# A graph layer on one core: loads first in SyncE's queue, norms of two blocks interleaved, early rows kept in later left factors

## The chip, the core and the metric

The kernel runs on one core of a Trainium2 chip. The metric is the device time of one execution in microseconds (us); the median of three runs before the change is 1426.39 us. A profile of one further execution is read beside it.

A core has several engines, each with its own queue of instructions that it works off in order: TensorE (PE; its weight loads are listed as PEld), VectorE (DVE), ScalarE (ACT), GpSimd (POOL) and SyncE (SP), which here only issues DMAs. An instruction that has to wait holds up everything behind it on its engine.

## The reference

```python
# x: (1250, 1024), 20000 edges (src -> dst, type 0..7), D = 1024
h = relu(layernorm(x))                     # per row, no scale or shift
u = h @ root + bias
for r in range(8):
    mask = (edge_type == r)
    sums = segment_sum(h[src] * mask, dst)
    cnt  = segment_sum(mask, dst)
    u = u + (sums / max(cnt, 1)) @ weight[r]
z = concat([u, h]) @ w_gate + b_gate
out = x + tanh(u) * z + h * (1 - z)
```

The data are float32. So 11 matrices of 1024 x 1024 are applied to 1250 rows: eight edge types, root, and the two halves of the gate.

## The kernel before, in words

The 1250 rows are ten blocks of 128 (the last has 98). Blocks i and i + 5 form a pair; NP = 5 pairs. One step multiplies one pair by one matrix, and there are 11 x 5 = 55 steps. A step is written as a two by two scheme with seven half-size products instead of eight, each of them four matrix instructions (two records apiece in the profile). The left operands of the seven products, `A11, A12, A22, S1, S2, S3, S4`, are seven slots of one tile `h_op[i]` for each pair; `transposed` (L171) fills the A slots by transposing h on TensorE into PSUM banks and copying (one half on ScalarE, one on VectorE, L179), and `left` (L183) forms S1 to S4 on VectorE. The right operands are sums of the matrix's four quarters; `make_t1` to `make_t4` (L157 to L169) form them on VectorE. `product` (L192) runs the seven products and their evacuations: with banks b and c, the first goes into b, and b is copied out by ScalarE (L210); the second goes into c (L213); the third is ADDED to what lies in b and copied out (L216); the fourth is added to c (L219 on VectorE); the fifth to b (L223, L224); the sixth has bank a (L228); the seventh is added to b (L231). After each product a function `between` may put other work into the queues; that is one turn of the generators below.

The engines' queues other than GpSimd's are in the order in which the Python program issues the instructions; the buffer pools add waits where a buffer is taken again.

The start: x is loaded by SyncE (`load_x`, L359) into three rotating buffers `xt`; `normed` (L366) takes the statistics of a block on VectorE (L370, L372), a square root on ScalarE (L374), the scale on VectorE (L376, L378) and a ReLU on ScalarE (L380), and stores h (L381); `with_h` (L383) adds h to x and stores the sum (L386), which frees the x buffer. h of pairs 0 to 3 is held in `lend`, two slots of the last pair's left factor, free until that pair is transposed. Pair 0 is done before the first step; the generator `norms` (L684) does pairs 1 to 4 during the first steps, 15 turns in all. Beside it the generator `columns` (L421) loads the edges, fills a table in memory and computes an integer key for every edge. After both, `slots` (L500) ranks the edges in 40 groups of up to 512 (two turns each; L534 and L585 on TensorE, L613 scatters to the table from GpSimd), and `order` (L630) sorts the nodes by their number of edges: L643 broadcasts 30 x 128 values, L667 compares them, and `rows_and_weights` (L331) writes the node order (L334), reads it back (L343) and gathers each node's slots (L298). From step 20 on, `edges` (L773) gathers result rows by GpSimd (L753) and adds them on VectorE (L761) between the products of later steps. Results of a step are stored by SyncE (L274) from four rotating buffers.

Of the kernel before, what the change touches and what calls it, by code (L numbers as in the profile page):

```python
# [19 lines left out]
def tile_rgcn_highway(  # L20
# [331 lines left out]
    with ExitStack() as early:  # L352
# [6 lines left out]
        def load_x(i, part):  # L359
            d = i + part * NP  # L360
            n = nrows(d)
            t = xpool.tile([P, D], F32, name="xt")
            nc.sync.dma_start(t[:n], x[d * P:d * P + n, :])
            return t

        def normed(xt, ht, d):  # L366
            n = nrows(d)
            st = xpool.tile([P, 2, 6], F32, name="st")
            for j in range(2):
                nc.vector.bn_stats(st[:n, j, :], xt[:n, j * Q:(j + 1) * Q])  # L370
            mv = xpool.tile([P, 2], F32, name="mv")
            nc.vector.bn_aggr(mv[:n], st[:n].rearrange("p a b -> p (a b)"))  # L372
            sd = xpool.tile([P, 1], F32, name="sd")
            nc.scalar.activation(sd[:n], mv[:n, 1:2], AF.Sqrt, bias=eps[:n])  # L374
            rs = xpool.tile([P, 1], F32, name="rs")
            nc.vector.reciprocal(rs[:n], sd[:n])  # L376
            less = xpool.tile([P, 1], F32, name="less")
            nc.vector.scalar_tensor_tensor(less[:n], mv[:n, 0:1], -1.0, rs[:n],  # L378
                                           op0=OP.mult, op1=OP.mult)
            nc.scalar.activation(ht[:n], xt[:n], AF.Relu, scale=rs[:n], bias=less[:n])  # L380
            nc.sync.dma_start(h_dram[d * P:d * P + n, :], ht[:n])  # L381

        def with_h(xt, ht, d):  # L383
            n = nrows(d)
            nc.vector.tensor_add(xt[:n], xt[:n], ht[:n])  # L385
            nc.sync.dma_start(xh_dram[d * P:d * P + n, :], xt[:n])  # L386


        lend = [h_op[NP - 1][:, 2 * part:2 * part + 2].rearrange("p a k f -> p (a k f)")
                for part in range(2)]  # L390
        xs = [load_x(0, 0), load_x(0, 1)]
        fac[0].load_first()
        fac[0].load_b22()
        fac[0].load_b21()
        xs.append(load_x(1, 0))
        for part in range(2):
            normed(xs[part], lend[part], part * NP)
        for part in range(2):
            transposed(h_op[0], part, lend[part], nrows(part * NP))
# [4 lines left out]
        left(h_op[0], 3)  # L404
        fac[0].make_t4()
        for part in range(2):
            with_h(xs.pop(0), lend[part], part * NP)
        xs.append(load_x(1, 1))


# [10 lines left out]
        def columns():  # L421
            with tc.tile_pool(name="ix0", bufs=1) as ix0:
                far = ix0.tile([P, G * ND * WIDE // 4], I32, name="far")
                nc.gpsimd.memset(far, FAR)
                for t in table.rearrange("(a p f) o -> a p (f o)", a=4, p=P):
                    nc.sync.dma_start(t, far)

                C2 = NCH - P
                ed, f = {}, {}
                for name, of, pad in (("dst", dst, G * KEYS), ("typ", etype, R), ("src", src, 0)):  # L430
                    t = ix0.tile([P, 2, P], I32, name=f"e_{name}")
                    nc.gpsimd.memset(t[:, 1, :], pad)
                    nc.sync.dma_start(t[:, 0, :], of[:P * P].rearrange("(c p) -> c p", p=P))
                    nc.sync.dma_start(t[:C2 - 1, 1, :],
                                        of[P * P:(NCH - 1) * P].rearrange("(c p) -> c p", p=P))
                    nc.sync.dma_start(t[C2 - 1:C2, 1, :EL], of[None, (NCH - 1) * P:])
                    ed[name] = t
                yield
                for name in ("dst", "typ", "src"):
                    f[name] = ix0.tile([P, 2, P], F32, name=f"f_{name}")  # L440
                    nc.vector.tensor_copy(f[name], ed[name])
                late = ix0.tile([P, 2, P], F32, name="late")
                nc.vector.tensor_single_scalar(late, f["typ"], float(R0[1]), op=OP.is_ge)
                for g in range(2, G):
                    nc.vector.scalar_tensor_tensor(late, f["typ"], float(R0[g]), late,
                                                   op0=OP.is_ge, op1=OP.add)
                key = ix0.tile([P, 2, P], F32, name="key")
                nc.vector.scalar_tensor_tensor(key, late, float(KEYS), f["dst"],
                                               op0=OP.mult, op1=OP.add)
                key_i = ix0.tile([P, 2, P], I32, name="key_i")  # L450
                nc.vector.tensor_copy(key_i, key)
                lo_i = ix0.tile([P, 2, P], I32, name="lo_i")
                nc.vector.tensor_single_scalar(lo_i, key_i, P - 1, op=OP.bitwise_and)
                for to, of in ((keys_dram, key_i), (los_dram, lo_i)):
                    nc.sync.dma_start(to[:P * P].rearrange("(c p) -> c p", p=P), of[:, 0, :])
                    nc.sync.dma_start(to[P * P:].rearrange("(c p) -> c p", p=P), of[:C2, 1, :])
                yield

                blk_i = ix0.tile([P, 2, P], I32, name="blk_i")
                nc.vector.tensor_single_scalar(blk_i, ed["dst"], 7, op=OP.arith_shift_right)  # L460
                blk = ix0.tile([P, 2, P], F32, name="blk")
                nc.vector.tensor_copy(blk, blk_i)
                row = ix0.tile([P, 2, P], F32, name="row")
                nc.vector.scalar_tensor_tensor(row, f["typ"], float(N), f["src"],
                                               op0=OP.mult, op1=OP.add)
                for g in range(1, G):
                    less = late
                    nc.vector.tensor_scalar(less, f["typ"], float(R0[g]),
                                            float((R0[g - 1] - R0[g]) * N),
                                            op0=OP.is_ge, op1=OP.mult)  # L470
                    nc.vector.tensor_add(row, row, less)
                tb = ix0.tile([P, 2, P], F32, name="tb")
                nc.vector.scalar_tensor_tensor(tb, f["typ"], float(ND), blk,
                                               op0=OP.mult, op1=OP.add)
                yield
                yield

                for of, to in ((key, key_col), (row, row_col), (tb, tb_col)):
                    p = bank()
                    nc.tensor.transpose(p[:, :P], of[:, 0, :], ident)  # L480
                    nc.tensor.transpose(p[:, P:P + C2], of[:C2, 1, :], ident[:C2, :C2])
                    nc.vector.tensor_copy(to, p[:, :NCH])
                yield
                kcol_i = ix0.tile([P, NCH], I32, name="kcol_i")
                nc.vector.tensor_copy(kcol_i, key_col)
                part_i = ix0.tile([P, NCH], I32, name="part_i")
                nc.vector.tensor_single_scalar(part_i, kcol_i, P - 1, op=OP.bitwise_and)
                nc.vector.tensor_single_scalar(less_lo, part_i, -1.0, op=OP.mult)
                nc.vector.tensor_single_scalar(part_i, kcol_i, 7, op=OP.arith_shift_right)
                nc.vector.tensor_copy(hi_col, part_i)  # L490
                nc.vector.tensor_single_scalar(first, key_col, float(WIDE), op=OP.mult)
                nc.gpsimd.iota(io, pattern=[[1, P]], base=0, channel_multiplier=0,
                               allow_small_or_imprecise_dtypes=True)
                nc.gpsimd.iota(pid, pattern=[[0, 1]], base=0, channel_multiplier=1,
                               allow_small_or_imprecise_dtypes=True)
                nc.vector.tensor_scalar(before, io, pid, None, op0=OP.is_lt)
                nc.vector.tensor_single_scalar(less_pid, pid, -1.0, op=OP.mult)
                yield
# [131 lines left out]
        def order():  # L630

            with tc.tile_pool(name="sort", bufs=1) as sp:
# [48 lines left out]
                for _ in range(3):  # L681
                    yield

        def norms():  # L684
            for i in range(1, NP):
                yield
                hs = []
                for part in range(2):
# [9 lines left out]
                if i < NP - 1:  # L698
                    for part, (xt, ht, d) in enumerate(hs):
                        transposed(h_op[i], part, ht, nrows(d))  # L700
# [400 lines left out]
```

## Time and profile before

| what | us |
|---|---|
| median of the runs | 1426.39 (1426.23 to 1426.68) |
| the profiled execution, its own time | 1420.9 |
| its span in the trace | 1419.1 |
| TensorE busy | 1369.2 |
| VectorE busy | 862.2 |
| GpSimd busy | 610.9 |
| ScalarE busy | 338.5 |

The mean granted clock of TensorE was 0.987 of full speed. In the profile a line such as L201 is a line of the kernel; a group's row names the tile written, the tiles read, the shape, the number of instructions and their duration. An arrow `<-` behind an idle time names what ended it. In the rows for stretches of time, the columns are the stretch, the busy time of PE, PEld, DVE, ACT and POOL, the granted clock, the share of the DMA engines that was busy, and GB/s.

### The profile page before, as it was taken

Reading aid. Unit: us, or ns where it says so; the run is one execution under the profiler, and the core shown is the slowest. Engines: PE = TensorE matmul, PEld = TensorE weight load, DVE = VectorE, ACT = ScalarE, POOL = GpSimd, SP = SyncE. Lnnn points to the kernel's source line nnn. Section 1 sums busy time; section 2 is a strip of 40 time slices with the busy share of each in tenths; the row PEclk is TensorE's granted clock in tenths of the full one; section 3 lists DMA queues with packets and bytes.
Section 4 is the critical chain, followed back from the end, with each engine's and each line's share of the span. In section 5 each row is a group of like instructions: output and inputs, shape, how many; then the busy total and the mean of one; then the engine's idle time right before and its main releaser. Section 6 shows DMA issues by size and latency. Waiting matters only on the chain.

```text
span 1419.1 us, 11950 instructions
## 1 busy us (share of the span) xinstructions
PE 1369.2 (96%) x3562; PEld 619.3 (44%) x3562; DVE 862.2 (61%) x1658; ACT 338.5 (24%) x718; POOL 610.9 (43%) x537
## 2 busy tenths in 40 slices
PE   5789999999999999999999999999999999999996
PEld 2344444444444444444444444444444444444442
DVE  5754877797768805077545663745446464567983
ACT  1234565566631111110101111111111111121210
POOL 0000665565561648474534343445425333324531
PEclk9799999999999999999999999999999999999998
DMA  7563765476646146467957655887769644557751
GB/s 253 202 223 96 154 170 128 109 174 161 134 101 195 35 76 150 120 227 272 320 206 242 230 188 186 277 317 254 252 250 321 219 149 169 192 180 270 265 162 56
DMA packets 109863, 272.73 MB, mean 192 GB/s; under 512 B 25890, under 2 KB 27920, under 8 KB 109664
## 3 DMA queue, kind: packets, MB, share of 16 engines
q0 software_dynamic: 48864, 128.60, 27.6%
q1 hardware_dynamic: 39808, 101.38, 23.9%
q10 hardware_dynamic: 21120, 41.95, 9.6%
q8 instruction: 28, 0.46, 0.2%
q14 instruction: 43, 0.35, 0.1%
HBM read 214.20 MB, written 80.65 MB: 208 GB/s over the span
## 4 chain that ended last, share of the span: by engine, by line
PE 80%; issue 6%; DVE 4%; DMA 1%; POOL 1%; ACT 0%; POOLq 0%; DVEq 0%; ACTq 0%
PE ps L201 79%; PE ps_n L534 1%; DVE row L1052 1%; DVE row L1053 0%; DMA got<-h_dram,node 0%; DVE w L990 0%; DVE h_op L990 0%; DMA y<-row 0%; PE ps_q L585 0%; DVE u L954 0%; PE ps L177 0%; POOL out_dram L303 0%; DVE row L228 0%; POOL got L298 0%; DVE u L761 0%
## 5 line engine op out<-in xcount | busy, mean ns | idle before, releaser
L201 PE MATMUL ps<-w,h_op 128*128 128x512 f32 x3080 | 1345.1, 596 | 1.0 <-ACT row L210 1.0
L201 PEld LDWEIGHTS ps<-w,h_op 128*128 128x128 f32 x3080 | 580.7, 191 | 695.7 <-issue 690.8
L753 POOL DMA_INDIRECT got<-y,idx x202 | 249.8, 1237 | 279.6 <-DVE u L761 226.1
L761 DVE SCALAR_TENSOR_TENSOR u<-got,w_of,u 128x1024 f32<-128x1024 f32 (+1 forms) x192 | 245.9, 1282 | 132.5 <-DMA got<-y,idx 130.4
L613 POOL DMA_INDIRECT table<-row_col,at_i x157 | 176.4, 1124 | 160.9 <-DVE at_i L609 68.5
L219 DVE TENSOR_TENSOR row<-row,ps 128x512 f32<-128x512 f32 x55 | 37.7, 686 | 164.7 <-PE ps L201 135.3
L223 ACT COPY part<-ps 128x512 f32<-128x512 f32 x55 | 32.1, 584 | 277.2 <-PE ps L201 269.7
L231 ACT COPY row<-ps 128x512 f32<-128x512 f32 x50 | 29.2, 584 | 259.7 <-PE ps L201 247.1
L224 DVE TENSOR_TENSOR row<-row,part 128x512 f32<-128x512 f32 x55 | 37.9, 689 | 65.5 <-ACT part L223 56.7
L210 ACT COPY row<-ps 128x512 f32<-128x512 f32 x55 | 32.1, 583 | 173.3 <-PE ps L201 155.0
L213 ACT COPY row<-ps 128x512 f32<-128x512 f32 x55 | 32.1, 583 | 137.4 <-PE ps L201 128.7
L216 ACT COPY row<-ps 128x512 f32<-128x512 f32 x55 | 32.1, 583 | 129.6 <-PE ps L201 126.9
L599 DVE SCALAR_TENSOR_TENSOR junk<-k_bc,key_col,before 128x128 f32<-128x128 int32 x157 | 54.9, 349 | 4.2
L334 POOL DMA_INDIRECT node_dram<-ids,pos_i x30 | 36.2, 1206 | 38.8 <-issue 38.2
L157 DVE TENSOR_TENSOR w<-w,w 128x2048 f32<-128x2048 f32 x11 | 25.3, 2298 | 44.7 <-PE ps L201 44.7
L228 DVE TENSOR_TENSOR row<-row,ps 128x512 f32<-128x512 f32 x55 | 37.6, 683 | 24.2 <-PE ps L201 22.5
L516 ACT ACTIVATE is_lo<-io,less_lo 128x128 bf16<-128x128 f32 x157 | 50.1, 391 | 0.8 <-DMA xh_dram<-xt 0.8
L539 DVE TENSOR_TENSOR seen<-seen,ps_n 128x110 f32<-128x110 f32 x157 | 42.1, 268 | 12.8 <-PE ps_n L534 8.1
L667 DVE SCALAR_TENSOR_TENSOR junk<-v_bc,val,one 128x1280 bf16<-128x1280 f32 x30 | 46.5, 1551 | 3.9 <-DMA v_bc<-val_dram 3.1
L303 POOL DMA_INDIRECT u_dram<-u,node x20 | 25.7, 1285 | 51.8 <-DVE u L761 38.3
L181 POOL MEMSET h_op<- 128x120 f32 x4 | 0.8, 200 | 89.0 <-DVE xt L385 88.8
L177 PE MATMUL ps<-ident,h_op 128*128 128x128 f32 x64 | 12.1, 351 | 27.5 <-ACT h_op L380 27.3
(153 smaller groups left out, 752.5 us busy)
## 6 DMA issues: line engine op xcount, KB each, us to landing
y<-row SPq DMA_DIRECT2D x72, 512.0 KB
w<-in_L_gnn_weight_dram ACTq DMA_DIRECT2D x28, 1024.0 KB
k_bc<-keys_dram SPq DMA_DIRECT2D x39, 256.0 KB
l_bc<-los_dram SPq DMA_DIRECT2D x39, 256.0 KB
w<-in_L_gnn_w_gate_dram ACTq DMA_DIRECT2D x8, 1024.0 KB
xt<-in_x_dram SPq DMA_DIRECT2D x9, 512.0 KB
xh_dram<-xt SPq DMA_DIRECT2D x9, 512.0 KB
hr_dram<-row SPq DMA_DIRECT2D x9, 512.0 KB
```

The costliest lines, as they stand in the source:

```text
L201: nc.tensor.matmul(b, aop[:, i, k, :], w.of[i][:, k, :], start=(fresh and k == 0), stop=(k == KQ - 1), skip_group_check=True)
L219: nc.vector.tensor_add(c12, c12, c)
L224: nc.vector.tensor_add(c22, c22, d)
L228: nc.vector.tensor_add(c11, c11, a)
L334: ins = nc.gpsimd.indirect_dma_start(out=node_dram[g][:, :], out_offset=bass.IndirectOffsetOnAxis(ap=pos_i[:, g, d:d + 1], axis=0), in_=id ...
L516: nc.scalar.activation(is_lo[:, i, :], io, AF.Abs, bias=less_lo[:, c0 + i:c0 + i + 1])
L539: nc.vector.tensor_add(seen[j][:, i, :], was, p[:, i, :])
L599: nc.vector.scalar_tensor_tensor(junk, o["k_bc"][:, i, :], key_col[:, c:c + 1], before, op0=OP.is_equal, op1=OP.mult, accum_out=rank[:, c: ...
L613: ins = nc.gpsimd.indirect_dma_start(out=table[:, :], out_offset=bass.IndirectOffsetOnAxis(ap=at_i[:n, i:i + 1], axis=0), in_=row_col[:n, ...
L667: nc.vector.scalar_tensor_tensor(junk, v_bc[:, g, :], val[:, c:c + 1], one.to_broadcast([P, KEYS]), op0=OP.is_gt, op1=OP.mult, accum_out=p ...
L753: nc.gpsimd.indirect_dma_start(out=t[:n], out_offset=None, in_=y[g][:, :], in_offset=bass.IndirectOffsetOnAxis(ap=at[:n, d, k:k + 1], axis=0),
L761: nc.vector.scalar_tensor_tensor(u[:n], t[:n], w, u[:n], op0=OP.mult, op1=OP.add)
```

## The change

SyncE's queue begins with x of pair 0, the first matrix's quarters with x of pair 1 put among them, one block of pair 2, then the edges and the table. The stores of h and of x + h come after them. x of pair 1 goes into `h_op[3]` (slots of pair 3's left factor) instead of the rotating buffers, and h of pair 1 into free slots of `h_op[4]` and `h_op[3]`. The norms of a pair's two blocks interleave (`both`): the second block's first statistics stand between the first block's square root and its scale. Pair 0's ReLU is issued in two halves, and a square root of a constant stands first in ScalarE's queue. The norm of pair 1 is issued before the first step; its transposes come after the first step's fifth product instead of its fourth. `norms` now takes 18 turns, and `columns` lets six turns pass before it begins to compute.

```diff
@@ the norm of a block in parts (stats, spread, scale, relu, store, with_x), and of two blocks @@
+        def both(a, b, parts=1):
+            a.stats(0)
+            a.stats(1)
+            a.spread()
+            b.stats(0)
+            a.scale()
+            a.relu(parts)
+            b.stats(1)
+            b.spread()
+            b.scale()
+            b.relu(parts)
+
+        def factored(i, blocks):
+            for part in range(2):
+                transposed(h_op[i], part, blocks[part].ht, blocks[part].n)
@@ the start @@
-        xs = [load_x(0, 0), load_x(0, 1)]
+        warm = xpool.tile([P, 1], F32, name="warm")
+        nc.scalar.activation(warm, eps, AF.Sqrt)
+        x0 = [load_x(0, part) for part in range(2)]
         fac[0].load_first()
         fac[0].load_b22()
+        x1 = [load_x(1, 0, scratch(NP - 2, 0))]
         fac[0].load_b21()
-        xs.append(load_x(1, 0))
-        for part in range(2):
-            normed(xs[part], lend[part], part * NP)
-        for part in range(2):
-            transposed(h_op[0], part, lend[part], nrows(part * NP))
+        x1.append(load_x(1, 1, scratch(NP - 2, 1)))
+        xs = [load_x(2, 0)]
...
+        b0 = [Normed(part * NP, x0[part], scratch(NP - 1, part)) for part in range(2)]
+        both(*b0, parts=2)
+        factored(0, b0)
         fac[0].make_t1()
         left(h_op[0], 1)
         fac[0].make_t2()
         fac[0].make_t3()
         left(h_op[0], 3)
+        b1 = [Normed(1 + part * NP, x1[part], scratch(NP - 1 - part, 2)) for part in range(2)]
+        both(*b1)
         fac[0].make_t4()
-        for part in range(2):
-            with_h(xs.pop(0), lend[part], part * NP)
-        xs.append(load_x(1, 1))
+        for b in b0 + b1:
+            b.store()
+        for b in b0:
+            b.with_x()
+        xs += [load_x(2, 1), load_x(3, 0)]
@@ columns: the loads of the edges and the table are issued above, before b0 @@
+            for _ in range(6):
+                yield
@@ norms @@
-            for i in range(1, NP):
+            for _ in range(4):
                 yield
...
+            factored(1, b1)
+            left(h_op[1])
+            yield
+            for b in b1:
+                b.with_x()
+            yield
+            for i in range(2, NP):
+                blocks = []
+                if i < NP - 1:
+                    blocks = [Normed(i + part * NP, xs.pop(0), scratch(NP - 1, part))
+                              for part in range(2)]
+                    both(*blocks)
                     yield
+                    for b in blocks:
+                        b.store()
                     yield
+                    factored(i, blocks)
+                    left(h_op[i])
+                    yield
+                    for b in blocks:
+                        b.with_x()
+                    xs.append(load_x(i + 1, 1))
+                    if i + 2 < NP:
+                        xs.append(load_x(i + 2, 0))
+                    yield
...
@@ index @@
-            for _ in zip_longest(columns(), norms()):
+            for _ in zip_longest(norms(), columns()):
                 yield
```

Line numbers in the prediction are those of the kernel before.

## The prediction

> **What bounds the kernel now.** I read the share of each engine first, then TensorE's waits, then windows of 5 us over the start, then the timelines of the places where TensorE stood. Page, parts 1 and 2:
>
> ```profile
> PE 1369.2 (96%) x3562; PEld 619.3 (44%) x3562; DVE 862.2 (61%) x1658; ACT 338.5 (24%) x718; POOL 610.9 (43%) x537
> PEclk9799999999999999999999999999999999999998
> ```
>
> TensorE is busy for 1369.2 of 1419.1 us, so only its 49.9 idle us and its slow clock can be won. By windows of 20 us it idles 9.2, 12.3, 5.4, 0.6, 4.2 and 2.6 us in the first 120 us (34.3), then hardly until the end. Who ends that idle time (TensorE's waits, 0 to 130 us: total, times, longest), and the windows (columns: span, busy of PE, PEld, DVE, ACT, POOL, clock, DMA):
>
> ```profile
> PE ps L177 <- ACT h_op L380: 27.3, 4, 14.8
> PE ps L177 <- ACT xt L380: 6.8, 2, 4.2
> 25.00:30.00 5.00, 2.72 (x7) 0.94 (x5) 2.46 (x3) 0.00 (x0) 0.00 (x0) 1.00 0.53 210
> 30.00:35.00 5.00, 0.00 (x0) 0.00 (x0) 0.00 (x0) 0.00 (x0) 0.00 (x0) 0.68 0.81 220
> 35.00:40.00 5.00, 0.00 (x0) 0.00 (x0) 3.50 (x10) 0.00 (x0) 0.00 (x0) 0.50 0.13 33
> 50.00:55.00 5.00, 5.00 (x13) 2.17 (x11) 2.78 (x6) 0.59 (x1) 0.00 (x0) 0.77 0.98 330
> ```
>
> All of it is transposes (L177) waiting for a normalised block (L380). The clock falls to half about 4.1 us after the last matmul (27.73; 0.68 in 30 to 35 puts the fall at 31.8) and returns 3.2 us after matmuls resume (49.13; 0.77 in 50 to 55 puts it at 52.3). Timelines (start, duration, engine; in brackets idle before):
>
> ```profile
> 5.69 1.28 ACT L374 ACT_TABLE_LOAD   x1 [5.69 <-DVE mv L372]
> 9.09 4.04 PE L177 MATMUL ps<-ident,h_op 128*128 128x128 f32 x16 [9.09 <-ACT h_op L380]
> 12.92 14.81 PE L201 MATMUL ps<-w,h_op 128*128 128x512 f32 x32
> 17.46 0.58 ACT L210 COPY row<-ps 128x512 f32<-128x512 f32 x1 [4.57 <-PE ps L201]
> 42.56 1.97 PE L177 MATMUL ps<-ident,h_op 128*128 128x128 f32 x8 [14.84 <-ACT h_op L380]
> 49.13 5.17 PE L201 MATMUL ps<-w,h_op 128*128 128x512 f32 x8
> 105.45 13.92 PE L201 MATMUL ps<-w,h_op 128*128 128x512 f32 x32
> 119.21 0.36 PE L534 MATMUL ps_n<-is_at,is_lo 128*128 128x110 bf16 x4
> ```
>
> TensorE is out of work at 27.73 and resumes at 42.56. One of the seven products of a step is 8 records, 3.45 us warm, 5.17 us from cold. Each ScalarE copy of a finished product (L210) runs as soon as the product is done. A later place has no margin either, and I weigh it because the change moves the index work:
>
> ```profile
> 458.69 1.55 POOL L334 DMA_INDIRECT node_dram<-ids,pos_i  x1 [29.85 <-issue]
> 594.82 1.02 POOL L753 DMA_INDIRECT got<-y,idx  x1 [0.30 <-issue]
> 598.99 1.28 DVE L761 SCALAR_TENSOR_TENSOR u<-got,w_of,u 128x1024 f32<-128x1024 f32 x1 [31.38 <-DMA got<-y,idx]
> 608.37 0.58 ACT L210 COPY row<-ps 128x512 f32<-128x512 f32 x1 [5.79 <-DMA y<-row]
> 609.01 16.58 PE L201 MATMUL ps<-w,h_op 128*128 128x512 f32 x38 [0.98 <-ACT row L210]
> ```
>
> GpSimd works without a wait on TensorE from 458.69 (first node rows) to 594.82 (fifth gather). VectorE stands in order behind that gather for 31.4 us; the row store behind it is late, so is the copy L210, and TensorE stops for 0.98 us. Margin: none.
>
> **The start.** The same ten x loads, ten h stores, ten x+h stores, nine edge loads and four table stores are issued; SyncE now puts x of block pairs 0 and 1, one block of pair 2, the edges and the table ahead of the stores. ScalarE gets one dummy square root, and two ReLUs become four halves. Bytes up to the last x of pair 1: 6.3 MB; at the 341 GB/s of the first 20 us, landed by about 18.5, before VectorE wants it.
>
> First block pair: the table load leaves the chain (row: 1.28 us, the square root follows at 6.98 at once). ScalarE: Activation LUTs, section What ACT_TABLE_LOAD costs, counts a drain of about 1.38 beside the load, 2.66 together; that would give 1.4 us more. The row decides: 1.28. Statistics of the second block lie beside the first's square root, and halves of ReLU let transposes begin at about 7.4. Last transpose 11.4, against 13.1; first product from 11.2 instead of 12.92 and, with the same ramp, over at 15.8. Second product to 19.25.
>
> Here stands a new wait. On ScalarE, both ReLUs of pair 1 now stand AHEAD of L210, and the third product accumulates into the bank that L210 reads. VectorE: right-factor and left-factor sums 12.1 to 21.2 (2.2 and 0.6 to 0.7 each, as at 13.77 to 22.9 before), statistics and scales of pair 1 to 25.85 (0.64 each, 0.21, 0.16, square root 0.3, with the second one behind the first ReLU of 1.24), so the second ReLU ends at 27.1, L210 at 27.7. Behind the ReLUs in ScalarE's queue stand L210, L213, L216 and matrix 1's first two loads; for L210 the third product waits, for L213 the fourth. Third product: 27.75 instead of 19.25. TensorE idles 8.5 us, goes cold, and the product takes 5.05 instead of 3.45.
>
> From there, chained: fourth 36.25, fifth 39.7 (ReLUs long done), 16 transposes 41.8, sixth 45.3, seventh 48.7. VectorE waits for the fourth product to 36.3, then follows with margin. Step 1: products to 55.65; transposes of pair 2 (its ReLUs end 54.3) to 57.75; third 61.2; six index transposes 1.24; fourth to sixth 72.8; transposes of pair 3 (last x load is issued 2.7 us after the x+h store of pair 2, as at 57.49 and 60.16 before, landing 69.2; second ReLU ends 73.5) to 74.9; seventh 78.35. Step 2: second product 85.25; 0.7 us wait for the ReLU of pair 4, whose target buffer is freed by a store; 87.0; fourth 93.9; transposes 94.65; fifth 98.1. That is where the row of 119.21 stands (19 products done): gain 21.1 us. Check from the other side: idle 25.1 after the first transposes, about 6.2 of slow clock (two sets and one of 8 transposes at 1.97 for 1.04, two products 1.7 over) and 1.7 of start are 33.0; less 8.5, 1.6 and 0.7 are 22.2. I take 21.1.
>
> The price of the moves on other queues: matrix 1's loads on ScalarE are issued near 33 instead of 46 and used a whole matrix later; GpSimd's fill of the short block waits nowhere that matters; stores at SyncE now wait behind loads, and their first reader comes in the gate.
>
> **The index.** Norms take 18 turns instead of 15 before the edge groups begin: the first group (L534) comes after 22 products, not 19; the last after 105, not 102. In TensorE's own time the chain to GpSimd is up to 10.3 us later. Worked on the time of before: last group's product at 433.2 instead of 422.4; VectorE is less behind, its result at 434.6 (before 426.8); last scatter and the wait for it to 440.1 (430.3): 9.8 late. Then the broadcast of 1.92 MB (L643), which landed 7 us after its issue at 433.33 with nothing beside it, is issued at 443.1, at the same time as the two 1 MB weight loads of ScalarE's queue (443.27). The row, alone on the engines, would add nothing. DMA: Bandwidth & Descriptors, section Queues, rings and completion order, says that each engine takes turns between its queues packet by packet, which speaks against the change here: shared equally, 1.9 MB beside 1.9 MB take about twice the 5 us of data, 4.5 more. The row would make the whole cost 9.8 + 1.6 = 11.4, the rule 15.9. No row of before has the two together; I take the middle, 2.2. Ten L667 follow, then the node rows: GpSimd's chain starts 12.0 late and ends 12.0 late. The margin being none, TensorE stops 12.0 us longer, and the clock falls: 1.6 more. Cost 13.6. TensorE doesn't wait between 119 and 608 otherwise, and what comes after is paced by it.
>
> Sum: 21.1 - 13.6 = 7.5 us off. Against the profiled execution, 1420.9 us (span 1419.1) to 1413.4; the runs' median, 1426.39, stands 5.5 above that, so 1418.9; I say 1419.
>
> **Rivals.**
> Cover holds: the index delay doesn't reach TensorE. It would need slack in GpSimd's chain; only its 29.85 us wait before 458.69 is slack, and that is for VectorE's places, which are late themselves. Then only the start counts: 1426.4 - 21.1 = 1405.3. Chance 0.17.
> The ScalarE order doesn't bite: the third product starts at 19.3. Then 10.1 more: 1409; with the first rival 1395. The order of ScalarE's queue speaks against it. 0.05.
> More waits at the start (pair 3's late x, VectorE with hardly any idle time between 12 and 30): 4 to 8 us lost, 1423 to 1427, about no change. 0.11.
> Slower: GpSimd's wait for its node-row scatters. For group 0 it was 3.65 us (473.3 to 478.2), for the others 12.0 and 10.3. Should group 0's become 12.0 at its new place, beside the row stores, with the broadcast shared equally (4.5), the chain is 9.8 + 4.5 + 8.3 = 22.6 us late, plus 1.6: 24.2 against 21.1, 1429.5. It decides from a chain 19.5 us late. 0.07.
>
> **How the numbers follow.** Forecast 0.60: 1419, its own range 1415 to 1423 (broadcast 0 or 4.5, the start 2 either way). The range for 8 in 10 takes in the first rival and the better of the second: 1404 to 1423.5. A measurement can tell 0.2%, 2.85 us, from none: faster below 1423.5, slower above 1429.2. Faster: 0.59 of the forecast, 0.22 of the first two; 0.01 of the forecast and most of the waits are the same; faster 0.81, same 0.11, slower 0.08.
>
> **What would show it.** First transposes near 7.4. In the start ONE TensorE gap of about 8.5 us from 19 to 28, ended by ScalarE's L210, with the clock at 0.5 by its end; no other gap over 1.5 us; first index matmul after 22 products. At GpSimd the fifth gather later relative to TensorE by 12, and a TensorE gap of about 13 us where 0.98 was. Wrong would be: no gap at 19 (the second rival), a gap of about 1 us at the gather (the first), or an end of GpSimd's chain over 19 us late (the last).

## The result, and the profile after

The changed kernel takes 1408.01 us (median of 6 runs, 1403.13 to 1412.53), the kernel before 1426.11 (6 runs, 1423.66 to 1426.68). The ratio is 0.9875 (95% interval 0.9853 to 0.9897): 18.1 us off, where 7.5 were forecast. The profiled run of the changed kernel took 1409.36 us (span 1407.5), that of before 1420.9.

Page of the changed kernel, parts 1 and 2:

```profile
PE 1369.5 (97%) x3562; PEld 617.6 (44%) x3562; DVE 862.2 (61%) x1658; ACT 339.0 (24%) x721; POOL 624.3 (44%) x537
PEclk8999999999999999999999999999999999999998
```

TensorE's busy time is what it was (1369.2); its idle time fell from 49.9 to 38.0 us. Its waits over the whole span (line waited for, total, times, longest):

```profile
PE ps L201 <- ACT row L210: 8.5, 2, 8.2
PE ps L177 <- ACT h_op L400: 7.8, 2, 7.6
PE ps L201 <- DVE row L228: 5.8, 1, 5.8
PE ps L902 <- DVE most L899: 2.1, 1, 2.1
PE ps L177 <- ACT xt L400: 0.8, 1, 0.8
PE ps_q L636 <- ACT to_lo L627: 0.3, 1, 0.3
```

Of 34.1 us of transposes that waited for a norm (L177, first two lines of before), 8.6 are left, and 7.6 of these are the very first block's. In their place stand two waits on products: L210 at the start and L228 at the fifth gather. Timelines of the changed kernel, TensorE and then ScalarE, over the start (start, duration, engine; in brackets idle before):

```profile
7.55 4.01 PE L177 MATMUL ps<-ident,h_op 128*128 128x128 f32 x16 [7.55 <-ACT h_op L400]
11.35 7.81 PE L201 MATMUL ps<-w,h_op 128*128 128x512 f32 x16
27.32 13.56 PE L201 MATMUL ps<-w,h_op 128*128 128x512 f32 x24 [8.16 <-ACT row L210]
40.72 1.91 PE L177 MATMUL ps<-ident,h_op 128*128 128x128 f32 x16
```

```profile
23.71 1.24 ACT L400 ACTIVATE h_op<-h_op,less,rs 128x1024 f32<-128x1024 f32 x1 [0.52 <-DVE less L393]
25.56 1.24 ACT L400 ACTIVATE h_op<-h_op,less,rs 128x1024 f32<-128x1024 f32 x1 [0.42 <-DVE less L393]
26.71 0.56 ACT L210 COPY row<-ps 128x512 f32<-128x512 f32 x1
27.17 0.58 ACT L213 COPY row<-ps 128x512 f32<-128x512 f32 x1
```

The first product was done near 15 (in the first experiment below, where nothing stands ahead of it, its copy runs at 14.99), but L210 stands behind pair 1's two ReLUs and runs at 26.71; the third product starts 0.6 us later. And the place at the fifth gather, where the trace of before had one wait of 0.98 us (GpSimd, VectorE and TensorE of the changed kernel):

```profile
448.40 1.55 POOL L334 DMA_INDIRECT node_dram<-ids,pos_i  x1 [30.11 <-issue]
581.52 1.02 POOL L823 DMA_INDIRECT got<-y,idx  x1 [0.30 <-issue]
585.93 1.28 DVE L831 SCALAR_TENSOR_TENSOR u<-got,w_of,u 128x1024 f32<-128x1024 f32 x1 [30.62 <-DMA got<-y,idx]
590.17 5.17 PE L201 MATMUL ps<-w,h_op 128*128 128x512 f32 x8 [5.77 <-DVE row L228]
595.68 44.90 PE L201 MATMUL ps<-w,h_op 128*128 128x512 f32 x104 [0.34 <-ACT row L210]
```

TensorE stops for 6.1 us and runs 5.17 for 3.45 behind that (the granted clock is 0.68 from 590 to 595).

**One yardstick for all traces.** I take as reference the copy L210 of the sixteenth step: 436.40 us in the trace of before, 416.21 in the changed kernel. Everything up to it is the start and the index's own waits. Behind it, copies follow each other by 24.03 us (in the last steps by 25.8), the same in all traces of this table, but for two places: the stop at the fifth gather (by how much the two intervals around it exceed 48.07) and the wait of 2.09 us behind L899, where the interval is 26.50, or 28.20 if the clock falls. So the time of a run is the reference, plus a constant (983.25 fits all), plus these two losses. The sum adds up the intervals that make up the time, so that it closes proves nothing by itself; what it shows is that the other intervals stay the same:

| trace | reference | fifth gather after it | stop there | loss at L899 | sum + 983.25 | run's time |
|---|---|---|---|---|---|---|
| before | 436.40 | 158.42 | 1.24 | 0 | 1420.89 | 1420.9 |
| before again, 1 | 436.58 | 158.66 | 4.34 | 0 | 1424.17 | 1424.19 |
| before again, 2 | 436.15 | 153.38 | 0 | 1.70 | 1421.10 | 1421.10 |
| before again, 3 | 435.93 | 159.30 | 4.67 | 0 | 1423.85 | 1423.86 |
| changed | 416.21 | 165.31 | 8.11 | 1.71 | 1409.28 | 1409.36 |
| changed again | 415.19 | 164.40 | 8.40 | 0 | 1406.84 | 1406.84 |

With the fifth gather up to 153.99 us after the reference no trace stops. From 158.42 on all stop, and TensorE's idle time grows about as the gather gets later: 0.98 us in the first trace (158.42), 5.32 in the second trace of the changed kernel (164.40), 21.84 in an experiment below (180.40). It is not exact: two repeats of before idle 2.39 and 2.47 us with the gather only 0.24 and 0.88 later than in the first. And behind a stop the clock falls or doesn't. TensorE in the first repeat, then its clock there in the first trace and in the first repeat:

```profile
610.59 29.86 PE L201 MATMUL ps<-w,h_op 128*128 128x512 f32 x65 [2.39 <-ACT row L210]
610.00:615.00 5.00, 5.00 (x13) 2.26 (x12) 4.96 (x6) 1.17 (x2) 3.36 (x2) 1.00 0.11 33
610.00:615.00 5.00, 4.41 (x7) 1.87 (x8) 3.80 (x4) 1.13 (x2) 2.45 (x3) 0.66 0.23 75
```

Half clock behind the gather doesn't occur in the first trace of before; it lasts 3.41 us in the first and third repeat and in the first trace of the changed kernel, 6.83 us in its second. Each 3.41 us of work at half clock cost 1.71.

### The profile page after: what moved, and what is told of

The parts are those of the page before. It is cut to its first block, busy times and chain, and to the rows that moved or that the text cites. A ratio compares the mean times of both kernels' runs of the same rounds, so it can differ in the third digit from the quotient of the medians.

```text
span 1407.5 us, 11960 instructions
## 1 busy us (share of the span) xinstructions
PE 1369.5 (97%) x3562; PEld 617.6 (44%) x3562; DVE 862.2 (61%) x1658; ACT 339.0 (24%) x721; POOL 624.3 (44%) x537
## 4 chain that ended last, share of the span: by engine, by line
PE 52%; issue 3%; DVE 2%; DMA 1%; POOL 1%; POOLq 0%; ACT 0%; DVEq 0%; ACTq 0%
PE ps L201 51%; DMA got<-y,idx 0%; PE ps L177 0%; DMA y<-row 0%; POOL out_dram L303 0%; DVE row L1122 0%; DVE u L831 0%; DVE w L1060 0%; DVE u L1024 0%; DVE w L1077 0%; DVE w L165 0%; DVE far_k L897 0%; DVE row L1123 0%; POOL got L298 0%; DVE row L228 0%
## 5 line engine op out<-in xcount | busy, mean ns | idle before, releaser
L823 POOL DMA_INDIRECT got<-y,idx x202 | 254.2, 1258 | 272.7 <-DVE u L831 215.6
L210 ACT COPY row<-ps 128x512 f32<-128x512 f32 x55 | 32.1, 583 | 175.6 <-PE ps L201 162.1
L334 POOL DMA_INDIRECT node_dram<-ids,pos_i x30 | 36.5, 1215 | 39.1 <-issue 38.8
L228 DVE TENSOR_TENSOR row<-row,ps 128x512 f32<-128x512 f32 x55 | 37.6, 683 | 21.1 <-PE ps L201 21.1
L298 POOL DMA_INDIRECT idx<-table,node_key x30 | 35.8, 1195 | 9.2 <-issue 6.1
L298 POOL DMA_INDIRECT u<-u_dram,node x20 | 20.3, 1015 | 39.4 <-DMA last_dram<-u 14.3
```

The lines of the kernel that those rows point to most:

```text
L228: nc.vector.tensor_add(c11, c11, a)
L298: nc.gpsimd.indirect_dma_start(out=to, out_offset=None, in_=of, in_offset=bass.IndirectOffsetOnAxis(ap=at, axis=0))
L823: nc.gpsimd.indirect_dma_start(out=t[:n], out_offset=None, in_=y[g][:, :], in_offset=bass.IndirectOffsetOnAxis(ap=at[:n, d, k:k + 1], axis=0),
```

## The experiments

Line numbers in waits are those of the kernel in question; the few edits shift them by some lines. A median less 983.25, less the reference of the kernel's trace (the mean of them for the two kernels with several, 436.27 and 415.70), is about what its runs lose at the two places; I use it to split a time in two. It takes the traced reference to hold for the runs without a trace, and a reference alone can differ by 1 us, so a loss found this way is worked out and not seen.

**The norm of pair 1 behind the second product.**

```
-        both(*b1)
-        fac[0].make_t4()
-        ... (stores, x+h of pair 0, two loads)
 def norms():
-            for _ in range(4):
+            yield
+            both(*b1)
+            fac[0].make_t4()
+            ... (the same stores, x+h and loads)
+            for _ in range(3):
                 yield
             factored(1, b1)
```

> The changed kernel with one thing moved: the norm of block pair 1 (with the fourth right factor, the stores and the x+h of pair 0 that stand behind it) is issued from the first step after its second product, so that on ScalarE the copies L210 and L213 stand ahead of its two ReLUs; nothing else moves. Theory (the queue of ScalarE held the third product): the wait of 8.16 us ended by L210 and the cold clock behind it (about 1.6) go; a wait of 1 to 1.5 us before the fifth product, whose bank is copied behind the ReLUs, comes in their place. The index work is paced by the products and moves with them. 8 to 9 us off the changed kernel's 1408.0: 1399 to 1400. Rival (VectorE is the limit, and its sums only move): the gap comes back at the fourth product, which needs the last sums, or at the sixth: 0 to 4 off, 1404 to 1408.

Measured: 1399.59 us (5 runs, 1397.31 to 1403.56), ratio 0.9826 (0.9802 to 0.9849), 8.4 less than the changed kernel. Timelines of this kernel, TensorE, then ScalarE:

```profile
11.32 14.36 PE L201 MATMUL ps<-w,h_op 128*128 128x512 f32 x32
27.29 3.70 PE L201 MATMUL ps<-w,h_op 128*128 128x512 f32 x8 [1.61 <-ACT row L216]
30.83 1.91 PE L177 MATMUL ps<-ident,h_op 128*128 128x128 f32 x16
```

```profile
18.85 0.58 ACT L213 COPY row<-ps 128x512 f32<-128x512 f32 x1 [3.27 <-PE ps L201]
25.52 1.24 ACT L400 ACTIVATE h_op<-h_op,less,rs 128x1024 f32<-128x1024 f32 x1 [0.42 <-DVE less L393]
26.67 0.56 ACT L216 COPY row<-ps 128x512 f32<-128x512 f32 x1
```

Four products run in one piece, and of the 8.16 us 1.61 are left, now for the fifth product. VectorE's part of the norm moves with it, but the second ReLU ends when it did (26.76, before 26.80); it only no longer stands ahead of L210. The transposes of pair 1 come at 30.83 instead of 40.72, the reference at 407.44 instead of 416.21. The queue order on ScalarE was the price, as the prediction had it, and VectorE was not the limit.

**The index three turns earlier in the changed kernel.**

```
 for j in range(ng + 3):
+                skip = False
 ...
                     if f is None:
-                        yield
+                        if skip or not 2 <= j < 5:
+                            yield
+                        skip = True
```

> The changed kernel with the edge groups three turns shorter: groups 2 to 4 of the slot loop take one turn instead of two, so the last group comes after about 102 products, as in the kernel before. The start is untouched. Theory (index late by three turns holds the fifth gather): GpSimd's first node rows start about 10 us earlier, TensorE's stop at the fifth gather (5.8 us behind L228, about 1.6 of slow clock) shrinks to 0 to 1: 6 to 7 off 1408.0, so 1401 to 1402. Rival (that stop varies from run to run and has nothing to do with the three turns): no change, 1408, with the stop at the gather still several us long.

Measured: 1405.22 us (6 runs, 1403.02 to 1409.24), ratio 0.9865 (0.9844 to 0.9886); its interval overlaps that of the changed kernel. Neither expectation. The trace shows why it decides nothing alone: packing the groups has waits of its own (2.3 us for VectorE's `seen`, 1.2 for ScalarE's `to_lo`, in all 3.5 at the reference, 419.71), and the stop at the gather is 5.5 (gather at 159.69), no longer 8.1. By the split, the losses are 1405.22 - 983.25 - 419.71 = 2.3, where the changed kernel has 1408.01 - 983.25 - 415.70 = 9.1: 6.8 won, 4.0 given back. In the trace itself the loss is 5.5, against 9.8 and 8.4.

**Three empty turns in the kernel before, and seven.**

```
+            for _ in range(3):
+                yield
             with tc.tile_pool(name="ix", bufs=2) as ix:
                 yield from slots(ix)
```

> The kernel before with three empty turns between the norms and the edge groups: the index is three turns later and nothing else changes. The prediction's own step (12.0 us later at GpSimd, no margin, 1.6 of clock) gives 13.6 more than before: 1426.1 to 1439.7. Theory from the two traces (the shared broadcast cost 0.7 and the lateness reaches the gather as 7 to 10): 7 to 11 more, 1433 to 1437. Rival (the stop at the gather varies by itself): within 2 us of the kernel before, 1424 to 1428.

Measured: 1428.41 us (19 runs, 1426.86 to 1432.1), ratio 1.0028 (1.0019 to 1.0037): 2.7 more than 1425.74, the kernel before on the same occasion. The prediction's own step (13.6) is refuted, and so are the 7 to 11 that I expected from two traces; the rival comes nearest, by its number. In the trace the first node row is 31.97 us after the reference, not 22.29, so 9.7 late; the fifth gather is at 164.76, only 6.3 late; the stop is 8.28, so 7.0 more from trace to trace.

The same with `range(7)`, a whole step:

> The kernel before with seven empty turns ahead of the edge groups, one whole step of 24.0 us, so that the row stores meet GpSimd's chain at the same places as before. Theory (the chain has a length that depends on where it meets the stores: 136 to 137 us here, 132 to 133 three turns late; all else is passed on): 22 to 26 us more than before, 1448 to 1452. Rival (most of any lateness is taken up, as the 2.7 us for three turns suggest): 6 to 8 more, 1432 to 1434.

Measured: 1443.18 us (4 runs, 1441.59 to 1445.39), ratio 1.0127 (1.0108 to 1.0146): 18.3 more than the 1424.87 of the kernel before on that occasion, between the two expectations. Its trace, TensorE:

```profile
625.60 5.10 PE L201 MATMUL ps<-w,h_op 128*128 128x512 f32 x8 [20.81 <-DVE row L228]
```

First node row 23.0 late, fifth gather 22.0 late (180.40), stop 23.77 against 1.24: 22.5 more from trace to trace, as the theory has it, but 18.3 more from median to median. So lateness does reach the fifth gather, nearly all of it after a whole step and two thirds of it after three turns. In both experiments the time grows about 4 us less from median to median than from trace to trace, which is what one expects if the kernel before usually stops longer than in the trace that I predicted from.

**The kernels again, for traces.**

> The kernel before, unchanged, for another trace. Theory A (its usual stop at the fifth gather is longer than the 1.24 us of the trace at hand, whose run was 5 us below the median): a run of 1424 to 1427 shows a TensorE wait of 2 to 4 us there, ended by L210 or L228, with a slow clock behind it, and a fifth gather 2 to 4 us later in TensorE's own time because GpSimd's three waits for its node-row scatters are longer than 26 us together. Theory B (the 5 us come from elsewhere): the wait there is 1.0 again.

> The kernel before again. Theory A: time and stop at the fifth gather go together one to one over these traces (plus about 1.7 where the clock falls). Theory B: the stop is the same in all of them while the times differ.

> The kernel before again. Theory A: as in the two runs ahead of it, time and stop go together. Theory B: they don't.

> The changed kernel, unchanged, for another trace. Theory A: the start is the same to 0.3 us (20.2 ahead of the kernel before at the nineteenth product), and what differs from its first trace (1409.4) is the stop at the fifth gather, 6.9 there, and the fall of the clock at the wait behind L899. Theory B: the start varies by several us.

The table above has them. Theory A holds in its first half: run time goes with the two losses, two of three repeats stop for some 4.5 us with a slow clock behind, and the references of before lie within 0.65 us of each other. Its reason doesn't hold: the gather is not 2 to 4 us later in these two, only 0.24 and 0.88. L210, which TensorE waits for there, starts 5.6 us after the issue of the row stores that it waits for, in the first trace 4.8. The start of the changed kernel varies by 1.0 (theory A said 0.3), and that is the clock: the third product starts at 27.32 and in the repeat at 26.99, and full speed returns at 33.39 and in the repeat at 31.19. Means of the references are 436.27 and 415.70: the start is worth 20.6 us. The four traced runs of before lose 1.2 to 4.7; its 24 timed runs of one occasion, 1421.82 to 1429.79 with median 1425.74, would by the same sum lose 6.2 in the middle (on two later occasions, medians 1424.87 and 1424.89, 5.4). Timed runs leave no trace, so that part is worked out and not seen.

**Where three turns went: GpSimd's third wait.** In the traces of before GpSimd waits longer for the third set of node-row scatters to land (L343), or for the small load behind it (L344), than in those of the changed kernel. ScalarE's two weight loads (L127, 2 MB) are issued at one place of the step. Kernel before; then its second repeat; then the changed kernel, whose loads are issued at 543.25 (GpSimd's rows, and the loads):

```profile
563.44 0.94 ACTq L127 DMA_DIRECT2D w<-in_L_gnn_weight_dram  x2
578.25 1.02 POOL L343 DMA_DIRECT2D node<-node_dram  x1 [10.26 <-DMA node_dram<-ids,pos_i]
581.45 0.25 POOL L344 TENSOR_SCALAR node_key<-node 128x10 int32<-128x10 int32 x1 [2.17 <-DMA node<-node_dram]
```

```profile
563.19 0.94 ACTq L127 DMA_DIRECT2D w<-in_L_gnn_weight_dram  x2
568.49 1.02 POOL L343 DMA_DIRECT2D node<-node_dram  x1 [5.64 <-DMA node_dram<-ids,pos_i]
576.16 0.25 POOL L344 TENSOR_SCALAR node_key<-node 128x10 int32<-128x10 int32 x1 [6.65 <-DMA node<-node_dram]
```

```profile
564.71 1.02 POOL L343 DMA_DIRECT2D node<-node_dram  x1 [5.28 <-DMA node_dram<-ids,pos_i]
568.16 0.25 POOL L344 TENSOR_SCALAR node_key<-node 128x10 int32<-128x10 int32 x1 [2.43 <-DMA node<-node_dram]
```

In before the last scatter is out at 568.0, behind the loads, and the two waits are 12.4 us; in the first and third repeat 15.0 and 15.6. In the second the last scatter went 0.3 us ahead of the loads, and only the small load behind it met them: 12.3. In the changed kernel the scatters come 16 us after the loads: 7.7, in its repeat 7.6, in the kernel with three empty turns 7.6. To try that, the loads alone were moved:

```
-            if i == 0 and j == 3:
+            if i == 0 and j == 6:
                 new.load_first()
```

In the kernel before:

> The kernel before with one thing moved: ScalarE issues the next matrix's first two loads (2 MB, L127) after the last product of the first step of a matrix instead of after the fourth, 10.3 us later. Theory C (in the kernel before GpSimd's third wait for its node-row scatters falls into these loads, 127 to 139 us after the reference copy, and takes 10 to 12.6 us instead of 5.2; three turns later it starts after them): here the wait ends before the loads, about 5 long, the chain from first node row to fifth gather is 130 to 132 instead of 136 to 137, and the stop at the gather is 0 to 1: 1419.5 to 1421.5. Rival D (the length of that wait is chance, or comes from the row stores): chain and time as before, 1424 to 1426.

In the changed kernel:

> The changed kernel with the same edit. Theory C: here the third wait, at 143 to 148.5 us after the reference copy, now falls into the loads (137 to 149), takes 9 to 12 instead of 5, and the stop at the gather grows by 4 to 7: 1412 to 1415. The same edit has opposite signs on the two kernels. Rival D: no change, 1407 to 1409.

Kernel before with later loads: 1427.46 us (22 runs, 1425.84 to 1429.61), ratio 1.0019 (1.0011 to 1.0026), so slower, where 1420 was expected. GpSimd and ScalarE in its trace:

```profile
580.83 1.02 POOL L343 DMA_DIRECT2D node<-node_dram  x1 [5.45 <-DMA node_dram<-ids,pos_i]
584.54 0.25 POOL L344 TENSOR_SCALAR node_key<-node 128x10 int32<-128x10 int32 x1 [2.69 <-DMA node<-node_dram]
584.67 0.93 ACTq L127 DMA_DIRECT2D w<-in_L_gnn_weight_dram  x2
```

At the gather all came as theory C said: both waits 8.1, chain from first node row to gather 131.5, gather at 153.98, no stop at all. But in the first step the later loads lengthen the transposes' waits for the norms (waits on L380 39.1 us in 8 places, before 34.1 in 6), and the reference comes at 443.90, 7.6 later. By the split, the losses are 0.3 where before has 5.4 on the same occasion. That the loads lengthen the third wait is shown, with a price at the start that I hadn't worked out.

Changed kernel with later loads: 1408.07 us (6 runs, 1403.67 to 1411.54), ratio 0.9879 (0.9856 to 0.9901), no change, where 4 to 7 more were expected. The two waits did grow, to 7.10 and 5.78 (12.9 against 7.7), but the loads were issued 2.6 us after the last scatter, and the load of group 1's rows no longer met other traffic (3.6 against 6.84), so the gather is at 165.44, where it was. The rival came by its number: the third wait does what theory C says, the chain as a whole not.

**Group 2's node rows behind group 0's gathers.** The order of GpSimd puts 35 us of row work ahead of the fifth gather; a copy of the node numbers that VectorE makes later sends it behind.

```
-    def rows_and_weights(g):
+    def rows_and_weights(g, ids=ids):
 ...
-                yield from rows_and_weights(g)
+                of = ids
+                if g > 1:
+                    of = small.tile([P, ND], I32, name="ids_late")
+                    nc.vector.tensor_copy(of, ids)
+                yield from rows_and_weights(g, of)
```

In the first experiment's kernel, in the changed kernel and in the kernel before:

> The first experiment (norm of pair 1 after the second product) and one thing more: the node rows of edge group 2 read a copy of the node numbers that VectorE makes in the middle of group 0's updates, so that on GpSimd all of group 0's gathers up to the 35th stand ahead of those rows, and the fifth gather no longer waits for some 35 us of row work. Theory (the stop at L228 is that row work): no L228 wait, 4.8 + 1.6 less than the 1399.6 of the first experiment: 1392 to 1394. Rival (the rows only stop the gathers later, at the 35th, and the row store with them): a new wait of TensorE near 700 us, 1397 to 1400.

> The changed kernel with the node rows of group 2 behind group 0's gathers, and nothing else. It takes the stop at the fifth gather away while the index stays three turns late. Theory: the whole cost of the gather stop in the changed kernel is what this gives back, about 6.9 by its trace: 1400 to 1402. Rival (the lateness costs elsewhere, and the stop is covered in most runs): 1405 or more.

> The kernel before with the node rows of group 2 behind group 0's gathers, and nothing else. It tells how long the kernel before usually stops at its fifth gather. Theory A (its profiled run, 5 us below the median, was a lucky one; the usual stop is some 3 to 6 with its clock): 4 to 6 less than before, 1420 to 1422, and the runs lie closer together. Theory B (its usual stop is the 1.24 us of its trace, and the 5 us come from elsewhere): 1 less, 1424 to 1425.

Measured: 1408.38 us (ratio 0.9884, 0.9868 to 0.9901), 1414.52 (0.9936, 0.9914 to 0.9958) and 1438.02 (1.0098, 1.0082 to 1.0114): 8.8, 6.5 and 13.2 slower than without the edit. No theory named these times; only the second rival's bound (1405 or more) holds. The stop at the fifth gather is gone in all three, but TensorE, in the kernel before with this edit:

```profile
811.05 0.37 PE L832 MATMUL ps<-ident,most 128*1 128x128 f32 x1 [17.80 <-DVE most L829]
```

VectorE reaches this reduction behind all of group 0's updates, and these now come late (the last at 807.3, before at 793.1): the wait of 2.1 us became 17.8 (18.3 and 15.0 in the other two). Moved behind the gathers, the row work is paid at the next place where TensorE needs VectorE. This order doesn't win the stop; what follows starts the chain sooner.

**Both, and the packed index.** The norm of pair 1 later, with six groups of the slot loop at one turn (`2 <= j < 8`):

> The changed kernel with both edits: the norm of pair 1 issued after the second product, and six groups (2 to 7) of the slot loop with one turn instead of two, so three turns ahead of the kernel before. Theory: the two gains add (8.5 and 6.5), and what is left of a stop at the gather in the kernel before goes too (1 to 5): 1388 to 1393. Rival (the gains overlap, or packing the groups makes TensorE wait for one-hot tiles or places): 1396 or more, with new waits before the index matmuls.

Measured: 1401.35 us (5 runs), ratio 0.984 (0.9818 to 0.9862). Stop and clock loss are 0 in its trace, and its run is the reference plus 983.25; but the packed groups wait 5.6 us for `seen` and 1.2 for `to_lo`, and the reference is 417.51, 10.1 behind the first experiment's. The rival holds: the gain at the gather is spent on packing.

**The chain sooner, at no turn's cost.** The first experiment, the later loads, and this in `places`, so that GpSimd scatters while VectorE still counts:

```
                         if d % 2:
+                            if g == 0:
+                                nc.vector.tensor_copy(pos_i[:, g, d - 1:d + 1], pos[:, d - 1:d + 1])
                             yield
-                    nc.vector.tensor_copy(pos_i[:, g, :], pos[:, g * ND:(g + 1) * ND])
+                    if g:
+                        nc.vector.tensor_copy(pos_i[:, g, :], pos[:, g * ND:(g + 1) * ND])
```

> The changed kernel with three edits: norm of pair 1 after the second product (the first experiment); the loads as in the two kernels ahead; and VectorE hands the places of group 0 to GpSimd two columns at a time instead of ten, so that GpSimd's first node-row scatters start some 13 us sooner. Theory: the chain is early enough for no stop at the fifth gather (before: none when it came 153.4 us after the reference copy; here about 152), so 8 less than the 1399.6 of the first experiment, and the wait behind L899 stays: 1390 to 1393. Rival (the scatters two at a time or the loads run into something else, and GpSimd is slower than its own sums): 1397 or more.

Measured: 1391.15 us (5 runs, 1389.57 to 1391.77), ratio 0.9758 (0.9737 to 0.9778), the fastest of all and the least scattered. Its trace, GpSimd and TensorE:

```profile
424.38 2.17 POOL L334 DMA_INDIRECT node_dram<-ids,pos_i  x1 [15.67 <-issue]
539.48 80.85 PE L201 MATMUL ps<-w,h_op 128*128 128x512 f32 x188
```

The first node row comes 17.7 us after the reference (32.2 in the changed kernel), the fifth gather at 152.72, and TensorE runs through. The later loads cost this kernel's start nothing (reference 406.64). How much of the earlier gather is owed to each of the two new edits is not separated; in the changed kernel the later loads alone left it at 165.44.

**Without the dummy square root.** `warm` is not computed, so the table load stands where it stood.

> The changed kernel without the dummy square root: the table load stands between the first statistics and the first square root again. By the row (1.28 us, next instruction at once) the first transposes come 1.3 us later, at 8.8 to 8.9 instead of 7.55; by the skill's 1.28 and a drain of 1.38 together they come 2.7 later, at 10.2. The third product waits for ScalarE's second ReLU in either case, so the wait ended by L210 is as long or a little shorter.

One run, 1409.74 us. ScalarE and TensorE:

```profile
5.78 1.28 ACT L388 ACT_TABLE_LOAD   x1 [5.78 <-DVE mv L387]
7.07 0.29 ACT L388 ACTIVATE sd<-mv,eps 128x1 f32<-128x1 f32 x1
8.75 3.96 PE L177 MATMUL ps<-ident,h_op 128*128 128x128 f32 x16 [8.75 <-ACT h_op L400]
28.47 12.80 PE L201 MATMUL ps<-w,h_op 128*128 128x512 f32 x24 [8.48 <-ACT row L210]
```

The transposes are 1.20 later, the row's 1.28 and not 2.66. The third product is 1.15 later too (28.47 for 27.32), but it and the two behind it take 12.80 us instead of 13.56, and the next transposes are 0.4 behind (41.12 for 40.72). Full speed returned at 33.02 here, 0.37 us sooner than in the first trace of the changed kernel though the product started later. The reference, 416.50, is within 1.3 us of both traces of the changed kernel: what the table load is worth at the end is less than the clock alone makes these traces scatter, and one trace doesn't size it.

## Why the prediction was right and wrong

- **First blocks.** Transposes predicted at 7.4, measured 7.55; first product at 11.2, measured 11.35. The row of 1.28 for the table load held against the rule of the Trainium skill (ScalarE: Activation LUTs, What ACT_TABLE_LOAD costs), whose drain of 1.38 no trace here shows.
- **The new wait.** 8.5 us predicted, ended by L210 behind both ReLUs: 8.16 measured, and the first experiment gives it back. Clock 0.50 from 25 to 30, as said. One size was off: I had full speed return 3.2 us after the product's start (1.6 us lost), it took 6.1 in the first trace and 4.2 in the repeat.
- **The start.** 21.1 us predicted, 20.6 measured over six traces. The waits behind it came too: 0.83 for pair 4 where 0.7 was predicted.
- **The index: this step failed.** "Cost 13.6" measures about 2.7 (three empty turns alone), and by the split the changed kernel loses 9.1 against 6.2 in the kernel before: 2.9. With the start that is 20.6 - 2.9 = 17.7, which is 1425.74 - 1408.01. From the first trace of before to the first of the changed kernel the stop grew by 6.9; the last 4 us between that and 2.9 are the base, (3). Three terms were mis-sized:
  - (1) The broadcast beside the weight loads: 2.2, halfway between 0 and the 4.5 that I had estimated from the rule of the Trainium skill (DMA: Bandwidth & Descriptors, Queues, rings and completion order). It landed in 7.76 us where it took 7.04: 0.7.
  - (2) "Starts and ends 12.0 late": the chain started 9.9 late and ended 6.9 late (by the repeat 6.0), since I took its length as fixed. A chain that starts later meets other traffic; its third wait left the weight loads (12.4 us down to 7.7). Ten small scatters and the load behind them take 12.3 to 15.6 us where they or it meet the loads (2 MB) in before, and 7.6 to 8.1 clear of them; no run shows how the DMA engines shared their time.
  - (3) "The margin being none", and the sum made against one trace. There was no margin, but that run stopped for 1.24 us at full clock, two of three repeats for 4.3 and 4.7 with the clock's 1.71 us in it, and the usual run for some 6 by the sum of times. So the step started from too good a base, and "the clock falls: 1.6 more" was in part there already. I had seen that the profiled run was 5.5 below the median, and carried that over as a constant instead of asking which wait it was.
- **The rivals.** The second (1409: the order of ScalarE's queue doesn't bite) came nearest by its number, by luck: its sign, no gap at 19, is refuted by the 8.16 us. Cover holds (1405.3) is next, and not by its reason: the delay does reach TensorE. The slower case expected group 0's wait to go from 3.65 to 12.0; it is 5.18.
- **Behind 608.** "What comes after is paced by it" was nearly right: the wait of 2.09 us behind L899 is as in before (L829 there), but in some traces the clock falls behind it.

Open: why the timed runs of before lose more than its four traces, and what lengthens its second wait for scatters (8.4 to 12.0 us, where the changed kernel has 4.9 to 5.3).

## What to carry to other kernels

Ask of every queue what stands ahead of an eviction: work moved forward on an engine may cost that engine nothing and still hold the bank of the next product. A chain of DMA waits on a second engine has no fixed length; before passing a delay through it one for one, look which transfers each of its waits meets now and which it would meet then. When the profiled run is off the median, find the wait that makes it so before summing against it, and measure from a fixed copy late in the kernel, so that a change's own gain and a stop downstream come apart.

## What the runs showed that I had not expected

- The same wait of 2.09 us behind L899 cost 1.70 us more in 6 of 15 traces, for the clock fell behind it (0.93 and 0.73 in two windows of 5 us in the changed kernel, 1.00 and 1.00 in its repeat). The clock's records in the traces show which. In the middle of every trace, half speed lasts a whole multiple of 3.41 us (a loss of 1.71 us each), and its changes lie on one grid of 3.41 us, which lies elsewhere in each trace. In the six traces 2.09 or 2.10 us of the idle time fell within one step of that grid, and the next step ran at half speed; in the nine others a border of the grid cut the wait, and at most 1.77 us lay in one step. So the place of the grid, which the kernel doesn't set, decides. The Trainium skill (TensorE: Matmul & The Clock Gate, What's actually happening) has a window of 3.4 us that runs freely, which agrees; but it asks for a whole idle window, and here 2.09 us of one were enough.
- A lateness of three turns cost 2.7 us and one of seven 18.3: far from proportional. Of three turns the chain took up 3.4 us (9.7 to 6.3), of seven 1.0 (23.0 to 22.0), since it meets other transfers when it is shifted; about 4 us of both are the base.
- Behind the reference, 983.25 us repeat to 0.1 us in nearly all traces of eleven different kernels (0.3 with seven empty turns): what scatters there, in the traces, is the stop at the fifth gather and the clock behind it and behind L899.
